# Relative-position attention with a binary feed-forward branch: pairs ordered by half of the query blocks, query and key halves taken straight from PSUM, operands loaded in pieces, first outputs spread over eight pairs

## The chip, the cores and the metric

The kernel runs on one core of one Trainium2 chip. The metric is the device time of one execution in microseconds (us); the time of a kernel is the median of several runs. The core has the engines PE (TensorE: matrix products into PSUM banks), DVE (VectorE), ACT (ScalarE), POOL (GpSimd) and SP (SyncE, which here only issues DMA transfers). Each engine works through its own instructions in order and waits at an instruction until the semaphores that it names are there.

## The reference

The input x is 16 sequences of 512 rows of 128 features. What is computed, cut to what matters:

```python
xn = layernorm(x)
q, k, v = xn' @ Wq + bq, xn' @ Wk + bk, xn' @ Wv + bv      # xn' = layernorm(xn) * g + b; 16 heads of 8
p = sinusoidal(512, 128) @ Wp
content = einsum("bihd,bjhd->bhij", q + u_bias, k)
pos = relative_shift(einsum("bihd,jhd->bhij", q + v_bias, p))
attn = softmax((content + pos) * 8 ** -0.5)
head = einsum("bhij,bjhd->bihd", attn, v)                  # 16 x 16 x 512 x 8
out = x + (head @ Wo + bo) + ffn(xn)
# ffn: [h, -h] @ (+1/-1 weights, 256x512), relu * 2, 512x512, relu * 2, 512x128, scaled by s0, s1, s2
```

## The kernel before

**Three stages.** A prologue computes the projections and the FFN for one sequence b after another and leaves what attention needs in DRAM scratch. An attention loop does all 16 heads. A tail multiplies the summed heads by Wo, adds the residual and stores.

**The prologue.** The FFN of sequence b is ffn_layer (products L640, splits L617 and L618), ffn_last (L674, into the bank a_t) and ffn_out (L685 to L691, which stores x + bo + FFN to res_scr). Between its steps the function more() pops a list of other steps at a fixed rate: norm (L318 to L339), transposed2 (L509, L620, L621), with_bias (L520), project_q (L545), project_k (L565), project_v (L575, L583), and next_quads at the end (L594 to L596). SPAN says over how many of the FFN's sequences the list is spread (12.3), XB how many tiles of x there are (4). PSUM has seven banks in turn: three for those steps (psw, names 0 to 2) and four for the FFN (F_BANKS). Queries and keys are kept as two f16 parts, a rounded one and the rest. A projection is first scaled and biased from PSUM into an f32 tile by ACT (scaled, L528), then halves_to makes the parts: ACT copies (L502) and POOL subtracts (L503).

```python
        def halves_to(src, hi, lo):
            nc.scalar.copy(hi, src)
            return nc.gpsimd.tensor_tensor(lo, src, hi, ALU.subtract)
```

The query tiles are zeroed by POOL (clear_queries, L496), since each 32-row group holds the queries of every second sequence only. ffn_residual loads x again and POOL adds the bias (L661, L662). When the list is empty, more() issues the stores of the query quads (L605, L606) and the loads of the first head.

**The attention loop.** A unit is four queries (of each of four blocks of 128 rows) of all 16 sequences for one head; 16 units make a pair, and two pairs, up = 0 and 1, make a head. Pairs are ordered by head and then by up, 32 in all. e_t holds the exponentials of two pairs in turn. A cycle does two units in the order of STEPS; A and B are score matmuls (scores, L797, L813, L826), F, G, H the maxima (L840, L845), T and N the transposed maxima (L850, L854), X and Y the subtraction of the maximum on PE and the exponential on ACT (L859, L869), V the products with the values for the pair before (weighted, L887, copied out at L896).

```python
STEPS = "N0- A0 B0 G1- H1- X0- F0 Y0- T1- N1- V G0 X1- A1 Y1- H0 T0 B1 F1"
```

In the attention loop, a manual schedule keeps PE, DVE and ACT in the order in which the program states their instructions. POOL and SP are ordered by the framework, which follows program order as far as buffers allow. The rules for what is issued between steps stand in the loop at the end:

```python
                nl = n // UL + 1
                if u % UL == 1 and 2 <= nl < len(loads):
                    if nl % NL == 0:
                        load_head(nl // NL)
                    load_queries(*loads[nl])
```

So every 8 units the queries for the next 8 are loaded into the buffer of the two that comes free (12 transfers of 64 KB: L216 for the content part, L220 and L224 for the two position parts), and every 32 units a head's keys, windows and values (load_head, L202, L205, L207, L208), always all at once.

**Sums and division.** At the end of half a pair, stored_sums (L921 to L931) writes the denominators to a small tile (den, L921) and the unnormalised sums to sum_scr (L926). Some cycles later inverted() takes the reciprocal (L929) and stores it (L931). Once per head divided() reads both back (L942, L943; the reciprocals broadcast to eight rows), multiplies on POOL (L946) and writes the quotients to head_scr (L947).

**The tail.** The last two pairs run last_steps: load_sums (L960) reads the quotients of all other heads, load_rden and divide (L963, L978) finish the first half of the last head, load_res (L970) reads the residuals. For the last pair last_sums multiplies by a selector matrix on PE, so that each denominator stands in the rows of its head (L904), then reciprocal and product on DVE (L906, L907), and last_moved moves the rows into the tile of sums (L914). output_of does four sequences at a time, eight times: products with Wo (L986), the add of the residual (L994), two stores (L997). In the last pair SP is in the manual order too.

The functions follow as they stand in the kernel; the line numbers are those of the profile.

## Time and profile before

| | |
|---|---|
| median of 3 runs | 1370.04 us (1368.51 to 1371.51) |
| the profiled execution | 1368.64 us |
| its span, first to last instruction | 1366.9 us |
| mean granted TensorE clock | 0.985 |
| PE busy | 1289.9 us (94%) |
| DVE busy | 1113.8 us (81%) |
| ACT busy | 882.3 us (65%) |
| POOL busy | 130.7 us (10%) |
| DMA packets, bytes | 243607, 160.22 MB |

The page gives the busy time of each engine over the whole span, and then in 40 slices of 34.2 us, where a digit is the busy share in tenths. A line of a timeline has the start in us from the first instruction, the duration, the engine (SPq is SP's own DMA queue), the line and operation, what is written and read, and in brackets how long the engine stood idle before it and what released it. A source row gives minimum, median and maximum of the durations in ns.

### The profile page before, as it was taken

The page shows a single profiled execution, that of the slowest core. Times are in us where ns is not written, and L with a number is a line of the kernel's source. Part 1 is how long each engine was busy: PE and PEld are TensorE (multiplying, and loading weights), DVE is VectorE, ACT ScalarE, POOL GpSimd, SP SyncE. Part 2 cuts the span into 40 slices and gives each one's busy share as a digit, 9 for nine tenths or more (in the row PEclk, how much of TensorE's full clock was granted, in tenths as well). Part 3 has the DMA queues.
Part 4 walks back from the last instruction along what each step waited for, and adds up shares of the span by engine and source line. Part 5 has one row for each costly group of instructions (what it writes and reads, how often), then busy time and mean ns, then how long its engine had stood idle before and what let it go on. Part 6 is the DMA issues. An engine that isn't in the chain of part 4 may idle for free. (4 is left out here: it accounts for less than half of the span.)

```text
span 1366.9 us, 55407 instructions
## 1 busy us (share of the span) xinstructions
PE 1289.9 (94%) x23061; PEld 952.7 (70%) x23061; DVE 1113.8 (81%) x2723; ACT 882.3 (65%) x1456; POOL 130.7 (10%) x115
## 2 busy tenths in 40 slices
PE   4988889979999999999999999999999999999966
PEld 2545555667777777777777777777777777777735
DVE  8988754678888888888888888888888888788846
ACT  4576668466666666666666666666666666666630
POOL 4243445010000000000000000000000000000011
PEclk9999999999999999999999999999999999999987
DMA  4597869863243323333333323332333353323288
GB/s 117 168 234 198 202 159 264 245 193 89 76 104 79 98 80 92 81 98 90 84 93 89 94 78 97 82 96 77 96 84 93 87 123 86 99 78 81 69 145 190
DMA packets 243607, 160.22 MB, mean 117 GB/s; under 512 B 79510, under 2 KB 227100, under 8 KB 243356
## 3 DMA queue, kind: packets, MB, share of 16 engines
q1 hardware_dynamic: 243356, 156.69, 43.9%
q8 instruction: 180, 2.95, 0.9%
q14 instruction: 71, 0.58, 0.2%
HBM read 96.34 MB, written 59.48 MB: 114 GB/s over the span
## 5 line engine op out<-in xcount | busy, mean ns | idle before, releaser
L869 ACT ACTIVATE e<-s,e_scale 128x512 f32<-128x512 f32 x1024 | 673.1, 686 | 319.9 <-PE s L859 319.5
L840 DVE TENSOR_REDUCE m<-s 128x256 bf16<-128x512 f32 x512 | 351.0, 686 | 132.0 <-PE s L826 131.9
L845 DVE TENSOR_TENSOR m<-s,m 128x256 bf16<-128x256 f32 x1024 | 428.5, 418 | 18.5 <-PE s L826 0.6
L797 PE MATMUL s<-q,k 128*128 128x64 f16 x8192 | 407.0, 193 | 4.0 <-DMA q<-qu_scr 2.1
L859 PE MATMUL s<-ident_b,nm 128*128 128x256 bf16 x2048 | 353.0, 275 | 2.3 <-DVE nm L854 2.3
L813 PE MATMUL s<-q,win 128*128 128x128 f16 (+1 forms) x4096 | 342.6, 206 | 0.0
L797 PEld LDWEIGHTS <-k 128*128 128x128 f16 x8192 | 334.3, 98 | 11.0 <-DMA q<-qu_scr 2.2
L887 PE MATMUL a_t<-e,v 128*9 128x256 f32 x4032 | 267.0, 382 | 0.7 <-ACT e L869 0.6
L813 PEld LDWEIGHTS <-win 128*128 128x128 f16 x4096 | 232.2, 98 | 0.2
L826 PE MATMUL s<-q,win_d 128*128 128x64 f16 x2048 | 227.7, 193 | 0.8 <-DMA q<-qv_scr 0.6
L859 PEld LDWEIGHTS <-nm 128*128 128x128 bf16 x2048 | 145.1, 98 | 117.2 <-DVE m L845 78.8
L854 DVE TENSOR_REDUCE nm<-t_t 128x2 bf16<-128x256 bf16 x512 | 208.8, 408 | 2.4 <-PE t_t L850 2.4
L887 PEld LDWEIGHTS a_t<-e,v 128*9 128x9 f32 x4032 | 86.5, 90 | 81.8 <-issue 2.5
L850 PE MATMUL t_t<-ident_b,m 128*128 128x128 bf16 x1024 | 141.0, 219 | 1.0 <-DVE m L845 0.9
L826 PEld LDWEIGHTS <-win_d 128*128 128x128 f16 x2048 | 130.2, 98 | 1.2 <-issue 1.1
L946 POOL TENSOR_TENSOR raw<-raw,rden 128x512 f32<-128x512 f32 x15 | 19.1, 1273 | 987.6 <-DMA rden<-rden_scr 762.8
L850 PEld LDWEIGHTS <-m 128*128 128x128 bf16 x1024 | 81.0, 97 | 32.7 <-DVE m L845 1.7
L640 PEld LDWEIGHTS <-e 128*128 128x128 f16 x512 | 49.5, 98 | 62.1 <-issue 14.8
L896 ACT COPY av<-a_t 128x256 f32<-128x256 f32 x126 | 47.0, 373 | 32.3 <-PE a_t L887 17.9
L618 DVE SCALAR_TENSOR_TENSOR h2l<-s,h2h 128x512 f16<-128x512 f32 x45 | 30.9, 686 | 37.0 <-ACT h2h L617 36.8
L640 PE MATMUL s<-h1l,e 128*128 128x512 f16 x180 | 47.1, 379 | 0.5 <-DVE h1l L618 0.4
L617 ACT ACTIVATE h2h<-s 128x512 f16<-128x512 f32 x45 | 26.9, 597 | 32.1 <-PE s L640 32.0
(176 smaller groups left out, 905.3 us busy)
## 6 DMA issues: line engine op xcount, KB each, us to landing
q<-qv_scr SPq DMA_DIRECT2D x512, 64.0 KB
q<-qu_scr SPq DMA_DIRECT2D x256, 64.0 KB
qu_scr<-k SPq DMA_DIRECT2D x32, 256.0 KB
k_scr<-hv SPq DMA_DIRECT2D x64, 128.0 KB
qu_scr<-win SPq DMA_DIRECT2D x32, 256.0 KB
qv_scr<-e SPq DMA_DIRECT2D x16, 512.0 KB
k<-k_scr SPq DMA_DIRECT2D x64, 128.0 KB
win<-p_scr SPq DMA_DIRECT2D x64, 79.5 KB
```

The costliest lines, as they stand in the source:

```text
L640: nc.tensor.matmul(ph, lhsT=w[:, t, f * P : (f + 1) * P], rhs=h[t][m], start=(m == 0 and t == 0), stop=(m == 1 and t == n - 1),)
L797: nc.tensor.matmul(sp[:, c % 2, :, :, 4 * g : 4 * g + 4].rearrange("p a r (n m) -> p n (a r) m", m=2), lhsT=kt[:, g, c * P : (c + 1) * P], ...
L813: nc.tensor.matmul(blocks[:, x0 : x0 + (NC + 1) * (len(cs) - 1) + 1 : NC + 1], lhsT=win[h % 2][:, side, y0 : y0 + P], rhs=qp[:, side, :, c ...
L826: nc.tensor.matmul(blocks[:, x0 : x0 + NC + 2 : NC + 1, 2 * t : 2 * t + 2], lhsT=win_d[h % 2][:, t, UP_OFF - 4 * u : WIND - 4 * u], rhs=qd ...
L840: nc.vector.tensor_reduce(st["m"], flat(st["ps"][0]).rearrange("p c x -> p x c"), AX.X, ALU.max)
L845: nc.vector.tensor_tensor(st["m"], flat(st["ps"][1])[:, c], st["m"], ALU.max)
L850: nc.tensor.transpose(st["pt"][:, f, :], st["m"][:, f * P : (f + 1) * P], ident_b)
L854: nc.vector.tensor_reduce(st["nm"], st["pt"], AX.X, ALU.max, negate=True)
L859: nc.tensor.matmul(flat(st["ps"][half])[:, :, f * P : (f + 1) * P], lhsT=st["nm"][:, f : f + 1].to_broadcast([P, P]), rhs=ident_b.unsqueez ...
L869: nc.scalar.activation(st["eT"][:, :, cs, :, i0 : i0 + 4].rearrange("p b c a r -> p (c a) b r"), st["ps"][half].rearrange("p c a r b -> p ...
L887: nc.tensor.matmul(bank[32 * r : 32 * r + VW, g], lhsT=v_t[h % 2][:, v0 : v0 + VW], rhs=pair["eT"][:, b, c], start=(c == 0 and (g == 0 or ...
L896: nc.scalar.copy(pair[half][:, g], bank[:, g])
```

## The change

1. **Order of the pairs.** All 16 heads' first half (up = 0) come first as pairs 0 to 15, then all second halves as pairs 16 to 31. Keys, windows and values are loaded for each pair, into buffers that alternate by pair. The score scratch, the reciprocals and the quotients hold one half at a time.
2. **Operands in pieces.** load_queries, and load_head without the values, return four pieces each; the loop appends them to a list and issues one piece per unit. The values come as one load at the fifth unit of a pair, from a scratch laid out by sequence and then head, which the prologue stores in one run per row.
3. **Content queries.** project_q does two sequences at once in two PSUM banks; qu_scr stores both in one row, so a row group's load also brings the other sequence's queries, and a POOL memset zeroes those right behind the load, in every piece.
4. **Halves from PSUM.** The weights are scaled once (q_mul, k_mul), ACT makes the rounded part with the bias from PSUM, and DVE makes the rest from PSUM (scalar_tensor_tensor; for the position queries in four pieces). The f32 tiles between, POOL's subtraction and two kinds of tile go. Banks: two for q, two for the other steps, three for the FFN. XB becomes 6 and SPAN 13.4. The residuals and the zeroing of the query tiles are placed elsewhere among the FFN's sequences.
5. **Division.** divided() works on one pair, half the size. Reciprocal, its store, the reads with the product, and the last store are four links; each F step of an even unit (one per cycle) runs the next link of every chain under way. For up = 0 and for the last seven heads the quotients go straight to the tile all_sums; for the first nine heads of the second half they go to early_scr and are loaded in one transfer later, as all_sums is in use.
6. **Outputs.** The first half's 16 sequences are done in pairs 17 to 24, two in each: the residual is loaded, two products with Wo go to one half of a_t (first_output), DVE adds into the residual's tile ("o", two buffers), two stores take it out, and the tile after next is loaded behind them. load_last reads the second half's residuals (2 MB) in pair 30. The last pair's denominators go through the selector as before, now also those of the second half of the pair before it; moved() and the output stores use SP's and ACT's queues, and eight calls of last_output end the kernel.

```diff
-    qu_scr = scr("qu_scr", [4, DH * H, B, S, 2], F16)
+    qu_scr = scr("qu_scr", [4, DH * H, B // 2, S, 2], F16)
...
-    v_scr = scr("v_scr", [P, H, B, NC * VW], F32)
-    sum_scr = scr("sum_scr", [H - 1, DH, B, 2, 2 * P], F32)
-    rden_scr = scr("rden_scr", [H, B, 2, 2 * P], F32)
-    head_scr = scr("head_scr", [P - DH, B, 2, 2 * P], F32)
+    v_scr = scr("v_scr", [P, B, H, NC * VW], F32)
+    sum_scr = scr("sum_scr", [H, DH, B, 2 * P], F32)
+    rden_scr = scr("rden_scr", [H, B, 2 * P], F32)
+    early_scr = scr("early_scr", [EARLY * DH, B, 2 * P], F32)
     res_scr = scr("res_scr", [B, S, D], F32)
-    Q_PARTS, K_PARTS = ((0, 2), (1, 3)), ((0, 1), (2, 3))
+    Q_PARTS, P_PARTS, K_PARTS = ((0, 3), (1, 2)), ((0, 2), (1, 3)), ((0, 2), (1, 3))
...
-    def load_head(h):
-        m = h % 2
+    def load_head(h, m):
...
-        nc.sync.dma_start(v_t[m], v_scr[:, h].rearrange("p b f -> p (b f)"))
+        return [lambda n=n: load(n) for n in range(4)]
+    def load_values(h, m):
+        nc.sync.dma_start(v_t[m].rearrange("p (b f) -> p b f", b=B), v_scr[:, :, h])
...
+        def load(n):
...
-                qu[:, n::4, 2 * l * P : 2 * (l + 1) * P],
-            )
+                qu[:, n // 2 :: 2, 2 * l * P : 2 * (l + 1) * P],
+            )
+            nc.gpsimd.memset(qc_t[m][rows_n, :, n // 2, :, 1 - n % 2], 0.0)
...
+        return [lambda n=n: load(n) for n in range(4)]
...
-        def psw(name, banks=(0, 1, 2)):
+        def psw(name, banks=(0, 1)):
...
-        XB = 4
+        XB = 6
...
-        SPAN = 12.3
+        SPAN = 13.4
...
-            nc.vector.tensor_scalar(q_mul, pw[:, 0:1], scale, None, ALU.mult)
+            for t, mul in ((wp_d, k_mul), (wq_d, q_mul), (wk_d, k_mul)):
+                nc.vector.tensor_scalar(t, t, mul, None, ALU.mult)
...
-        def halves_to(src, hi, lo):
-            nc.scalar.copy(hi, src)
-            return nc.gpsimd.tensor_tensor(lo, src, hi, ALU.subtract)
+        def halves_to(src, n, hi, lo):
+            nc.scalar.activation(hi, src, AF.Identity, bias=b_cols[:, n : n + 1])
+            for r in range(4) if len(src.shape) == 4 else [slice(None)]:
+                nc.vector.scalar_tensor_tensor(
+                    lo[:, r], src[:, r], b_cols[:, n : n + 1], hi[:, r], ALU.add, ALU.subtract
+                )
...
+            for n in range(2):
+                nc.tensor.matmul(
+                    q_banks[:, n],
+                    lhsT=wq_d,
...
+            halves_to(q_banks.rearrange("p n j -> p j n"), 0, *qu)
             for m in range(2):
                 for part in Q_PARTS[m]:
-                    nc.sync.dma_start(qu_scr[part, :, b], qu_b[n][m])
...
+            halves_to(
+                q_banks.rearrange("p n (q r) -> p r q n", r=4), 1, *[q[:, :, :, b : b + 2] for q in qv_all]
+            )
...
+            halves_to(pk, 2, *hv)
+            for m in range(2):
+                for part in K_PARTS[m]:
+                    nc.sync.dma_start(k_scr[part, :, b, :], hv[m])
...
-            nc.sync.dma_start(v_scr[:, :, b, :], vb.rearrange("p h c w -> p h (c w)"))
+            nc.sync.dma_start(v_scr[:, b], vb.rearrange("p h c w -> p h (c w)"))
...
-                if b + n + (RB if b else 0) < B:
-                    ffn_residual(b + n + (RB if b else 0))
+            for n in ((0, 1), (2, 3))[b] if b < 2 else (b + 2,):
+                if n < B:
...
-        def last_moved(pair, half, rs):
-            for r in rs:
+        def moved(pair, half, gs, engines):
+            for r in range(4):
                 b = 8 * half + 2 * r
-                nc.sync.dma_start(sums[1][L0:L1, b : b + 2], pair[half][32 * r : 32 * r + DH])
+                engines[r % len(engines)].dma_start(
+                    all_sums[rows_of_head(pair["h"]), b + gs[0] : b + gs[-1] + 1],
+                    pair[half][32 * r : 32 * r + DH, gs[0] : gs[-1] + 1],
+                )
...
             def inverted():
                 nc.vector.reciprocal(den, den)
-                inv = rden_scr[h, bs, up]
-                nc.sync.dma_start(inv.rearrange("b (q m) -> b q m", q=16), den)
-                if h == H - 1:
-                    load_rden(half)
-                elif up == 1 and half == 1:
-                    divided(h)
+                return inverse_stored() if n == 2 * H - 2 else inverse_stored
+            def inverse_stored():
+                nc.sync.dma_start(rden_scr[h, bs].rearrange("b (q m) -> (b q) m", q=16), den)
+                if half == 1:
+                    return lambda: divided(pair, B)
+                if n == 2 * H - 2:
+                    return lambda: divided(pair, B // 2)
...
+            nc.sync.dma_start(raw, sum_scr[h, :, :nb])
+            nc.sync.dma_start(rden, rden_scr[h, :nb].unsqueeze(0).to_broadcast([DH, nb, 2 * P]))
             nc.gpsimd.tensor_tensor(raw, raw, rden, ALU.mult)
-            nc.sync.dma_start(head_scr[h * DH : (h + 1) * DH].rearrange("w b u i -> w b (u i)"), raw)
+            if up and h < EARLY:
+                dst = early_scr[h * DH : (h + 1) * DH]
+            else:
+                dst = all_sums[rows_of_head(h)]
+            def stored():
+                nc.sync.dma_start(dst[:, :nb], raw)
+            return stored
...
+        def load_first(b):
+            if b < B:
+                first_res[b] = wk.tile([P, 2 * P], F32, tag="o", name=f"o_{b}")
+                res_rows(first_res[b], 0, b)
+        def products(dst, b):
...
+        def first_output(b, free):
+            products(a_t[:, free], b)
+            def added():
+                t = first_res.pop(b)
+                nc.vector.tensor_tensor(t, a_t[:, free], t, ALU.add)
+                res_rows(t, 0, b, store=True)
+                load_first(b + 2)
+            return added
...
+        def last_output(b0, step):
+            out_banks.append(out_banks.pop(0))
+            po = out_banks[-1].rearrange("p (b i) -> p b i", b=2)
+            bs = slice(b0, b0 + step + 1, step)
+            for x in range(2):
+                products(po[:, x], b0 + step * x)
+            nc.vector.tensor_tensor(last_res[:, bs], po, last_res[:, bs], ALU.add)
+            for b in (b0, b0 + step) if step > 1 else (slice(b0, b0 + 2),):
+                b = b if step == 1 else slice(b, b + 1)
+                for m in range(2):
+                    (nc.sync, nc.scalar)[m].dma_start(
+                        half_rows(out, 1, m, b),
+                        last_res[64 * m : 64 * m + 64, b].rearrange("p b (k d) -> p (b k) d", d=D),
+                    )
...
-        loads = [(h, l) for h in range(H) for l in range(NL)]
-        units, pairs, later, due, filled = {}, {}, [], [], []
+        loads = [(h, 2 * up + l) for up in range(2) for h in range(H) for l in range(2)]
+        units, pairs, later, due, filled, loading, outputs = {}, {}, [], [], [], [], []
...
-                if u % UL == 1 and 2 <= nl < len(loads):
-                    if nl % NL == 0:
-                        load_head(nl // NL)
-                    load_queries(*loads[nl])
+                if n % UL == 1 and 2 <= nl < len(loads):
+                    loading += load_queries(*loads[nl])
+                if n % UP == 1 and nl + 1 < len(loads):
+                    loading += load_head(loads[nl + 1][0], (n // UP + 1) % 2)
+                if n % UP == 4:
+                    loading.append(lambda h=h, m=n // UP % 2: load_values(h, m))
+                if loading:
+                    loading.pop(0)()
+                if n % 2 and outputs:
+                    filled.append(first_output(*outputs.pop(0)))
...
-                if due and n % 2 == 0:
-                    due.pop()()
+                if filled and n % 2 and n > UP * H:
+                    filled.pop()()
+                if n % 2 == 0:
+                    due = [more for more in (do() for do in due) if more]
...
+                k, pair = k[0], pairs[n]
+                if n == 2 * H - 2 and k == 3:
                     manual.close()
                     manual.enter_context(tc.manual_schedule(engines=ORDERED | {mybir.EngineType.SP}))
+                if n == 2 * H - 1 or (n == 2 * H - 2 and k == 7):
+                    due = [more for more in (do() for do in due) if more]
+                if n == 2 * H - 1 and k == 0:
+                    last_sums(pairs[n - 1], 1, 1)
+                    moved(pairs[n - 1], 1, (0, 1), [nc.sync])
...
+                    weighted(pair, 2 * k + m)
+                if n == 2 * H - 1:
+                    if k % 2 == 0 and k:
+                        last_sums(pair, *divmod(k // 2 - 1, 2))
+                    continue
+                if k == 0 and n == H + 1:
+                    load_first(0)
+                    load_first(1)
+                if k % 4 == 3 and H < n < H + 9:
+                    outputs.append((2 * (n - H - 1) + k // 4, 0))
+                if k == 1 and n == H + 11:
+                    nc.sync.dma_start(all_sums[: EARLY * DH], early_scr)
+                if n < 2 * H - 2:
+                    if k % 4 == 2 and later:
                         due.append(later.pop(0))
-                    if k[0] % 4 == 3:
...
+                    if k % 4 == 3:
+                        later.append(stored_sums(pair, k // 4))
+                elif k in (2, 4):
+                    due.append(later.pop(0))
+                elif k == 3:
+                    later.append(stored_sums(pair, 0))
+                    load_last()
+                elif k == 6:
+                    last_sums(pair, 1, 0)
...
+        moved(pair, 0, (0, 1), [nc.sync, nc.scalar])
+        last_output(0, 1)
+        last_sums(pair, 1, 1)
+        moved(pair, 1, (0,), [nc.sync, nc.scalar])
+        last_output(2, 1)
+        moved(pair, 1, (1,), [nc.sync, nc.scalar])
+        last_output(4, 1)
+        last_output(6, 1)
+        for b in (8, 12, 9, 13):
+            last_output(b, 2)
```

## The prediction

> **What bounds the kernel now.** I read the forty slices of the page first, then busy times by window, the waits, and the timeline of the places that they point at.
>
> ```profile
> PE   4988889979999999999999999999999999999966
> DVE  8988754678888888888888888888888888788846
> ACT  4576668466666666666666666666666666666630
> DMA  4597869863243323333333323332333353323288
> ```
>
> There are three stages. A prologue (projections and FFN) runs up to the first score matmul at 263.9 us (first start of L797). The attention loop runs from the first exponential at 270.4 to the last at 1315.0 (L869): 1044.6 us for 256 cycles of two units. A tail of 51.9 us remains.
>
> ```profile
> 800.00:900.00 100.00, 100.00 (x2094) 77.41 (x2090) 86.60 (x206) 68.72 (x113) 1.27 (x1) 1.00 0.33 87
> 1320.00:1325.00 5.00, 0.42 (x8) 0.00 (x0) 0.00 (x0) 0.00 (x0) 0.00 (x0) 1.00 1.01 162
> 1325.00:1330.00 5.00, 0.00 (x0) 0.00 (x0) 0.00 (x0) 0.00 (x0) 3.05 (x1) 0.51 0.70 128
> ```
>
> Columns: window, length, busy PE, PEld, DVE, ACT, POOL, clock, DMA share, GB/s. In the loop PE is never idle; DVE and ACT have room. A cycle is 4.03 us (score-value steps, L887, start at 1284.76, 1288.79, 1292.83), so a PE microsecond added there costs one, and one that a load comes late costs one. In the tail PE is empty for 10 us while the queues are full:
>
> ```profile
> 1323.86 0.30 SPq L963 DMA_DIRECT2D e<-rden_scr  x1
> 1324.90 0.61 SPq L921 DMA_DIRECT2D den<-av  x1
> 1331.07 0.25 DVE L929 RECIPROCAL den<-den 128x16 f32<-128x16 f32 x1 [17.55 <-DMA den<-av]
> 1333.08 1.19 PE L904 MATMUL t_t<-av,sel 128*128 128x256 f32 x2 [12.66 <-DVE e L906]
> ```
>
> SP stood until 1323.86 for a reciprocal written behind megabytes of reads; the denominators behind it went late, DVE's in-order queue stood 17.6 us for them, and PE 12.7 us for DVE.
>
> **Base of the sum.** The profiled execution took 1368.64 us, 1.7 more than its span, and lies 1.4 below the median. I sum changes on it and add them to the median.
>
> **Tail: -24.** The second half alone is left for the end. Gone are the reads of summed heads (about 2 MB each half) and of 2 MB of residuals inside the tail, half of the 128 output passes (L986, 7.3 us for 64), half of the 4 MB of stores, and the denominators of the second to last pair as a DMA. Followed from the last exponential (ends 1315.7): eight value steps of 0.96 us and three selector matmuls of 0.56 fill PE to about 1325. DVE's reciprocal and multiply (1.74 + 0.43, L906, L907) need one bank each time, so the second pair of them ends near 1323. The moves of that half are issued on two queues (0.65 us each) and land about 2 us later, near 1326.5. Eight outputs of 0.92 us PE and 0.69 us DVE follow, the last waiting for its own move: last add near 1337.5, two issues, 2 to 4 us to land: 1341 to 1343. That is 26 to 28 us against 51.9. I take -24; ends -18 (the 2 MB of residuals, read 20 us ahead, still hold up the moves) and -30.
>
> **First outputs inside the loop: +7.3.** 16 blocks of two fp32 products, 4 passes of 0.114 us: 7.3 us on the full PE. The add of 128x256 (0.42, row L845) fits DVE's idle 0.5 us per cycle; without that cover it costs up to 6 more.
>
> **Operands for every pair: +27.** k, win and win_d are now read 32 times, not 16, v in runs of 144 bytes. The DMA share (0.33) carries it: 17 ns for such a packet in the writes of before, 2048/16 of them 2.2 us. Here a rule speaks against the change. The row: a 64 KB query load takes SP 0.43 us and about 2.0 us to land (worked out from the semaphore times), eight in flight. The Trainium skill (DMA: Bandwidth & Descriptors, Bandwidth) wants transfers of 1 MiB and calls those under 64 KB dominated by descriptors; the Anatomy section gives each some 2 us of fixed cost. If that added up, 13 more transfers per pair would cost 26 us of 32; by the row they cost SP 6 us, beside PE. I take the row: bandwidth isn't the limit, the order in SP's queue is.
>
> ```profile
> 804.96 0.30 SPq L216 DMA_DIRECT2D q<-qu_scr  x1
> 808.07 0.58 SPq L921 DMA_DIRECT2D den<-av  x1
> 808.70 1.52 SPq L926 DMA_DIRECT2D sum_scr<-av  x4
> 810.27 0.31 SPq L224 DMA_DIRECT2D q<-qv_scr  x1
> 821.08 0.30 SPq L216 DMA_DIRECT2D q<-qu_scr  x1
> 837.12 0.61 SPq L943 DMA_DIRECT2D rden<-rden_scr  x1
> 841.69 1.27 POOL L946 TENSOR_TENSOR raw<-raw,rden 128x512 f32<-128x512 f32 x1 [62.54 <-DMA rden<-rden_scr]
> ```
>
> A query buffer comes free at R = 804.96 and its next content is needed 16.1 us later (821.08 is the other buffer's release). Before, loads went out at once. After, as the changed program is built, SP holds ahead of the second set of each pair the denominators (R+3.1) and four sums (to R+5.3), then v 0.6, the first quarter 1.4, the reciprocal's store 0.7, two quarters 2.9, the raw sums 0.5: the read of the reciprocals is issued at R+11.3, the last quarter ends near R+13.3. POOL stands for that read, with the last quarter's zeroing queued behind its multiply, and PE's next scores wait for the zeroing. Issue to multiply was 4.6 us for 256 KB; half the data I take at 3.9. Then 0.65 (half of 1.27) and 0.53 for 512 zeros (row L496): R+16.4 plus a semaphore, 0.4 us late. Ends: nothing (one microsecond better anywhere), 1.5 (v's small runs hold those behind them). 22 pairs without outputs: 8.8.
>
> In eight pairs two output stores and two residual reads enter the same chain. The reads take the buffer that the store has just left, so SP waits for its landing, which lies behind v: 1.0 + 1.0 us and a wait of 1 to 2. With PE's own 0.46 taken off, the last quarter is some 2.7 us late (ends 1 and 4): 21.6. Of before's own late loads (cycles of 4.5 to 4.6 us at every fourth load) about 3 go. Together 8.8 + 21.6 - 3 = +27.
>
> **Prologue: +3, start of attention +1.** Halves are taken from PSUM: ACT loses the three scalings of a block (0.78 to 0.81, L528), POOL all of L503 (63 us), DVE gains per block k 0.60, qu 0.57, qv 4 x 0.34 / 2 (the pace of such rows back to back): 1.85, 30 us in all, in a stage where it is 84 to 90% busy for the first 150 us. What it gets back is its blocking by POOL:
>
> ```profile
> L332 DVE TENSOR_SCALAR step<-step x16: 162/170/3332, 7.2 to 172.7; 128x8 f32<-128x8 f32 x16
> L335 DVE TENSOR_SCALAR xn<-xn,st,root x64: 326/339/1698, 7.9 to 176.5; 128x128 f32<-128x128 f32 x64
> ```
>
> Minimum, median, maximum: the maxima lie under POOL instructions. Durations above the median sum to 37 us over all DVE rows, 21 of them under L503 and L492, which go. The Trainium skill (SBUF — State Buffer, Who interferes with whom) says that a two-port DVE instruction and a GpSimd one exclude each other for the whole of it: by the rule up to 67 us of L503 and L492 could come back, by the row 21. I take 21, so DVE has 9 us more. The queue is spread over 67 calls, not 61.5, and FFN has three banks, not four; the PE-bound end (10.5 us a block from 231) becomes shorter. I take +3; ends -8 (the ACT-POOL chain goes from PE's waits) and +12 (DVE-bound throughout). The loads of the first unit follow next_quads, which moves from 31 us ahead of FFN's end to some 20; copies, eight stores and 12 loads took 25 in a full queue, fuller than it will be: +1, ends -1 and +5. Zeroing of 4 us on POOL and the q tiles' clearing are off the path.
>
> **Sum.** -24 + 7.3 + 27 + 3 + 1 = +14.3 to +14.8: 1383 on the profiled run, 1385 on the median. So the tail's gain is paid back in 30 small waits.
>
> **Rivals.** (a) Faster: the last quarter lands in time. The mechanism is the same chain, SP to POOL to PE, at the ends of the pairs; it decides at zeroing finished by R+16.1, that is reciprocals back within 3.3 us and a residual read that doesn't wait for its store. For it: 128 KB is half of what took 4.6 us, and before's last query issue at R+14 (851.23, needed at 853.3) did no harm. Against: eight pairs have 3 us more in the chain. -24 + 7.3 + 3 + 1 = -13: 1357 (1348 to 1366). (b) Every pair 1.5 us late, since v's small runs push all behind them: 22 x 1.5 = 33 in place of 8.8: 1409. (c) The prologue is held by DVE: +12 in place of +3: 1394, for it 84 to 90% busy before, against it the freed ACT and POOL.
>
> **Numbers.** The forecast case 0.47 (1374 to 1396), (a) 0.33, (b) 0.12, (c) 0.08. Predicted 1385. 1352 to 1404 leaves out the best fifth of (a) and most of (b), under 2 in 10. About 0.2% (2.7 us) is what a measurement of this kernel can tell from no change: 0.06 lies within it, where only part of the waits comes; faster 0.32, slower 0.62.
>
> **What would show it.** Tail from last exponential to end 26 to 28 us. In the waits, PE's score matmul on POOL's zeroing, some 0.4 us in ordinary pairs and 2 to 3 us in pairs 17 to 24; cycles of 4.03 elsewhere. DVE maxima of L332's kind down, first score matmul at 260 to 276. The prediction is wrong if cycles at pair ends stay at 4.03 (then (a)), or if the first score comes beyond 276.

## The result and the profile after

The changed kernel takes 1477.2 us (median of 4 runs, 1472.1 to 1485.66) against 1369.28 us before: 1.079 times as long, 95% interval 1.0756 to 1.0823. The profiled execution took 1485.66 us, with a span of 1483.9. By stages of the two profiled executions (the line numbers from here on are those of the changed kernel unless said otherwise):

| stage | before | after | difference | forecast |
|---|---|---|---|---|
| up to the first exponential | 270.4 | 251.1 | -19.3 | +4 |
| first to last exponential | 1045.3 | 1199.5 | +154.2 | +34 |
| last exponential to the end | 51.2 | 33.2 | -18.0 | -24 |
| span | 1366.9 | 1483.9 | +117.0 | +14 |

So the prologue is better than forecast, the tail somewhat worse, and the loop loses 154 us. Three rows of the page's forty slices:

```profile
PE   6899998899899999999999999898898899979996
DVE  8899666787687778777877787676777778867774
PEclk9999999999999999999999999999999999989998
```

PE no longer shows an unbroken row of nines in the loop. The waits say for what:

```profile
PE s L801 <- POOL q L218: 98.5, 29, 8.5
```

Score matmuls (L801) waited 98.5 us in 29 places for POOL's zeroing of the content queries (L218). With two waits on other releasers there are 31 gaps of PE before L801, 102.4 us; before the change there were four, 4.0 us. All but one stand at the first scores of a pair. Pairs are counted here by their exponentials; the outputs, which the change's pairs 17 to 24 hold counted by their values, then stand in pairs 18 to 25. Here is one wait, at the end of pair 9:

```profile
607.69 0.64 SPq L960 DMA_DIRECT2D rden<-rden_scr  x1
608.44 0.39 SPq L214 DMA_DIRECT2D q<-qu_scr  x1
...
611.31 0.72 POOL L961 TENSOR_TENSOR raw<-raw,rden 128x256 f32<-128x256 f32 x1 [2.77 <-DMA rden<-rden_scr]
612.45 0.66 POOL L218 MEMSET q<- 32x512 f16 x1 [0.41 <-DMA q<-qu_scr]
...
613.16 0.39 PE L801 MATMUL s<-q,k 128*128 128x64 f16 x8 [3.15 <-DMA sums<-raw]
```

The reader is to see the chain: the read of the reciprocals leaves SP at 607.69, ahead of the last piece of the queries; POOL stands for it until 611.31, then multiplies, then zeroes, and PE starts 0.05 us after the zeroing ends (the releaser that the PE line names is a transfer of the same moment). PE had been ready at 610.01. What the wait then costs is in the windows around it (length, busy PE, PEld, DVE, ACT, POOL, granted clock, DMA share, GB/s):

```profile
600.00:610.01 10.01, 10.01 (x210) 7.71 (x202) 8.34 (x20) 7.09 (x12) 2.02 (x3) 1.00 0.53 119
610.19:613.60 3.41, 0.44 (x12) 0.54 (x13) 0.92 (x3) 0.00 (x0) 1.38 (x2) 1.00 0.22 60
613.60:617.01 3.41, 3.41 (x42) 2.11 (x38) 1.98 (x5) 1.27 (x2) 0.00 (x0) 0.50 0.14 32
```

PE is busy again from 613.16, but for 3.41 us the granted clock is 0.50, and 42 matmuls run where some 72 would at the pace of the first row. The pair lasted 37.2 us: 32.2 + 3.15 of waiting + 1.8.

**The sum of the loop.** PE waited 102.4 - 4.0 = 98.4 us more. The cycles with a first output last 4.56 us instead of 4.03 (the eight that no low clock touches), 16 times: 8.5. Of 154.2 us 47.3 are left, 1.5 for each of the 31 waits: the low clock behind them. The clock's own records agree: in the loop it stood at 0.50 for 112.6 us, worth 56.3 us of full clock, against 3.4 us before; part of that fell on time in which PE stood anyway.

### The profile page after: what moved, and what is told of

The parts are those of the page before. It is cut to its first block, busy times and chain, and to the rows that moved or that the text cites. A ratio compares the mean times of both kernels' runs of the same rounds, so it can differ in the third digit from the quotient of the medians.

```text
span 1483.9 us, 56292 instructions
## 1 busy us (share of the span) xinstructions
PE 1332.5 (90%) x23065; PEld 976.8 (66%) x23065; DVE 1131.3 (76%) x2793; ACT 852.5 (57%) x1399; POOL 230.6 (16%) x340
## 3 DMA queue, kind: packets, MB, share of 16 engines
q8 instruction: 181, 2.97, 0.9%
## 4 chain that ended last, share of the span: by engine, by line
PE 63%; SPq 11%; DMA 10%; DVE 8%; POOL 3%; issue 3%; ACT 1%; POOLq 0%; DVEq 0%; ACTq 0%
PE a_t L890 13%; PE s L863 13%; PE s L801 13%; PE s L817 9%; DMA rden<-rden_scr 7%; PE p L626 5%; PE s L830 3%; PE t_t L854 3%; SPq L223 2%; SPq L219 2%; SPq L214 2%; DVE m L844 1%; POOL raw L961 1%; POOL q L218 1%; DVE m L849 1%
## 5 line engine op out<-in xcount | busy, mean ns | idle before, releaser
L801 PE MATMUL s<-q,k 128*128 128x64 f16 x8192 | 413.9, 195 | 104.0 <-POOL q L218 98.5
L801 PEld LDWEIGHTS <-k 128*128 128x128 f16 x8192 | 342.6, 99 | 112.8 <-issue 55.0
L863 PE MATMUL s<-ident_b,nm 128*128 128x256 bf16 x2048 | 364.0, 281 | 2.5 <-issue 1.6
L817 PE MATMUL s<-q,win 128*128 128x128 f16 (+1 forms) x4096 | 348.3, 209 | 0.0
L218 POOL MEMSET q<- 32x512 f16 x256 | 171.5, 670 | 930.6 <-DMA q<-qu_scr 756.0
L890 PE MATMUL a_t<-e,v 128*9 128x256 f32 x4032 | 280.0, 397 | 0.0
L854 PEld LDWEIGHTS <-m 128*128 128x128 bf16 x1024 | 85.9, 100 | 35.0 <-DVE m L849 4.9
L626 PE MATMUL p<-h1l,e 128*128 128x512 f16 x240 | 63.3, 383 | 0.0
L603 ACT ACTIVATE h2h<-p 128x512 f16<-128x512 f32 x60 | 35.7, 597 | 47.1 <-PE p L626 43.8
L626 PE MATMUL p<-h1h,e 128*128 128x512 f16 x240 | 62.2, 379 | 0.0
```

The lines of the kernel that those rows point to most:

```text
L218: nc.gpsimd.memset(qc_t[m][rows_n, :, n // 2, :, 1 - n % 2], 0.0)
L626: nc.tensor.matmul(ph, lhsT=w[:, t, f * P : (f + 1) * P], rhs=h[t][m], start=(m == 0 and t == 0), stop=(m == 1 and t == n - 1),)
L801: nc.tensor.matmul(sp[:, c % 2, :, :, 4 * g : 4 * g + 4].rearrange("p a r (n m) -> p n (a r) m", m=2), lhsT=kt[:, g, c * P : (c + 1) * P], ...
L817: nc.tensor.matmul(blocks[:, x0 : x0 + (NC + 1) * (len(cs) - 1) + 1 : NC + 1], lhsT=win[side_m][:, side, y0 : y0 + P], rhs=qp[:, side, :, ...
L854: nc.tensor.transpose(st["pt"][:, f, :], st["max"][:, f * P : (f + 1) * P], ident_b)
L863: nc.tensor.matmul(flat(st["ps"][half])[:, :, f * P : (f + 1) * P], lhsT=st["nm"][:, f : f + 1].to_broadcast([P, P]), rhs=ident_b.unsqueez ...
```

## The experiments

Theory Q: the order in SP's and POOL's queues makes the waits, and the clock doubles part of them. Rivals: the transfers themselves are slow (B), or POOL's zeroings are the cost (Z). All edits are to the changed kernel, but for e13.

**e1: the division's reads two cycles later.**

```diff
-                    return lambda: divided(pair, B)
+                    last = lambda: divided(pair, B)
+                    return (lambda: lambda: last) if n < 2 * H - 3 else last
```

> The reads and the multiply of the division run two cycles later in every pair but the last three, behind the last piece of the queries. Theory Q (the order in SP's and POOL's queues makes the wait): in the changed kernel's trace the last zeroing always starts when the multiply ends, 0.7 us ahead of PE; without the two reads (1.1 us of issue) and the multiply, the last piece lands some 2.5 us earlier, the 31 stalls of PE fall from 3.3 us to 0.5 to 1, and with them most of the 1.7 us of half clock behind each: about 1375 us (1360 to 1400). Rival B (the transfers themselves are slow, from twice the keys and small runs of the values): the last piece still lands late, 1450 us or more.

Measured 1384.06 us; waits of PE before L801 34.0 us in 19 places, those for POOL:

```profile
PE s L801 <- POOL q L218: 12.0, 7, 5.2
```

Theory Q holds; nothing about the transfers was changed but their order. What is left lies mostly (19.6 us) in pairs 18 to 25.

**e2: the values behind the queries.**

```diff
-                if n % UP == 4:
+                if n % UP == 9:
                     loading.append(lambda h=h, m=n // UP % 2: load_values(h, m))
```

> The values are appended behind the four pieces of the queries instead of ahead of them. Theory Q: the issue of the values (0.6 us) and the wait for a free slot right behind it (about 1 us) leave the chain, stalls fall by some 1.6 us to 1.7, in all 1477 - 31 x (1.6 + 0.5) = about 1412 us (1395 to 1435). Rival B (the small runs of the values hold the queries' packets in the DMA engines): landing of the queries falls by 2 us as well, stalls nearly go, 1370 us or less.

Measured 1379.85 us, better than expected. Pairs 1 to 17 all last 32.2 or 32.3 us; the 28.0 us of waits left before L801 stand in pairs 18 to 25, but for two in pair 0 and one in pair 28. I had overlooked that the edit does two things: the pieces of the queries are now stated one unit earlier, so the reads of the division come behind the last piece as well. It is e1 and e5 that take the two apart.

**e3: no zeroing.**

```diff
-            nc.gpsimd.memset(qc_t[m][rows_n, :, n // 2, :, 1 - n % 2], 0.0)
```

> The zeroing of the other sequence's content queries is left out, so the scores mix two sequences; everything else runs. Theory Q: PE then waits for the last position queries (issued 3.5 us ahead of its start, about 2.2 us to land) instead of for POOL: stalls fall by 1.2 us to 2.1, 1477 - 31 x 1.5 = about 1430 us (1415 to 1450). Rival Z (256 zeroings of 0.67 us on POOL are the cost): stalls nearly go, about 1350 us.

Measured 1451.85 us: 73.9 us of waits remain, now mostly for the loads of the queries themselves (54.6 us). POOL's zeroings are not the cost (Z falls); the last piece is late by itself. The gain was smaller than I expected.

**e4: transposes without a use in the wait.**

```diff
+                if n % UP == 0 and n:
+                    for f in range(24):
+                        nc.tensor.transpose(t_t[:, 2, f % 2], ident_b, ident_b)
```

> 24 transposes without a use (some 3.1 us of PE) are put ahead of each pair's first scores, where PE stands 3.3 us. Theory C (each stall costs twice: the granted clock is 0.50 for 3 us behind it): PE has almost no idle time there, the clock stays at 1.0, and the loop is shorter by up to 31 x 1.6 = 50 us: about 1435 us (1425 to 1450). Rival: the low clock has another cause, and the transposes only fill the wait: 1477 us, or some us more where the stall was shorter than 3.1.

Measured 1464.07 us: the gain is 13, not 42. The 24 transposes took 1.5 us, not 3.1 (with 0.4 of idle time ahead of them), so PE still stood in most pairs. But the clock:

```profile
core 0: 1460.5 us, clock 0.984
```

It was 0.957 in the changed kernel's profile. PE's waits, transposes counted as such (31 x 1.89 + 52.7), came to 111.3 us; of the loop's 129.3 us over before, 107.3 are waits, 8.5 outputs, and 13.5 are left for the clock where 47.3 were (by the clock's records 15.4 us of full clock, where 56.3 were). So the low clock follows from PE standing idle. What is left comes with idle times of 2 to 8 us that stayed behind the transposes, in pairs 18 to 24 and 28 above all. The waits grew by 9 us, part of it in pairs that would have waited less than the transposes take.

**e5: the values in long runs.** The scratch's old layout: loads in runs of 2304 bytes.

```diff
-    v_scr = scr("v_scr", [P, B, H, NC * VW], F32)
+    v_scr = scr("v_scr", [P, H, B, NC * VW], F32)
...
-        nc.sync.dma_start(v_t[m].rearrange("p (b f) -> p b f", b=B), v_scr[:, :, h])
+        nc.sync.dma_start(v_t[m].rearrange("p (b f) -> p b f", b=B), v_scr[:, h])
...
-            nc.sync.dma_start(v_scr[:, b], vb.rearrange("p h c w -> p h (c w)"))
+            nc.sync.dma_start(v_scr[:, :, b], vb.rearrange("p h c w -> p h (c w)"))
```

> Only the scratch of the values goes back to its old layout: loads in runs of 2304 bytes, stores of the prologue in runs of 144. Theory Q: the wait for a free slot behind the values' load (about 1 us) goes, the rest of the chain stays: stalls from 3.3 to 2.3 us, part of them then short enough not to bring the low clock (so far stalls of up to 2.1 us cost 0.2 us more than their length, longer ones 1.8): about 1425 us (1405 to 1445), the prologue within 3 us. Rival B (the small packets hold everything): 1390 us or less.

Measured 1427.33 us, as Q expected. The waits of the ordinary pairs (1 to 17, 26, 27, 29 and 30) have a mean of 1.3 us instead of 2.6: the small runs are part of the delay, by what they do to the transfers right behind them. SP's first issue behind the values takes 0.54 us on average instead of 1.47.

**e6: POOL subtracts again.** halves_to fills an f32 tile from PSUM by ACT, copies, and POOL subtracts.

```diff
-            nc.scalar.activation(hi, src, AF.Identity, bias=b_cols[:, n : n + 1])
...
+            nc.scalar.activation(t, src, AF.Identity, bias=b_cols[:, n : n + 1])
+            nc.scalar.copy(hi, t)
+            nc.gpsimd.tensor_tensor(lo, t, hi, ALU.subtract)
```

> The rest of each half is made by POOL again, from an f32 tile that ACT fills from PSUM (and the tile of the keys' halves has two buffers, as before, to make room); scaled weights, list, spread and banks stay as changed. Theory P (the 18.5 us that the prologue gained come from taking the chain from ACT to POOL and its blocking of DVE out): first score matmul at 258 to 268 instead of 245.4, the total 12 to 20 us longer, 1490 to 1497 us. Rival L (the longer spread of the list, more tiles of x and other banks did it): first score at 243 to 250, total 1477.

Measured 1501.3 us, first score matmul at 273.1: 27.7 us later than in the changed kernel, more than the 18.5 it had gained. The direction is P's; the size is not clean, as one f32 tile stands where before had three.

**e7: first outputs on ACT's queue** (with e2's edit). Stores and reads of res_rows use nc.scalar; reads wait three steps.

```diff
-                load_first(b + 2)
+                reads.append(b + 2)
...
+                if k % 4 == 2 and reads:
+                    load_first(reads.pop(0))
```

> The values behind the queries as in the run that did that alone; the first outputs' stores and residual reads are issued by ACT's queue, and a tile's next read comes some three cycles behind its store instead of at once. Theory Q: SP's queue loses 5.2 us of issue in the pairs with outputs, and the 28 us of stalls and some 10 us behind them that were left in pairs 17 to 25 go, but for PE's own 0.46 us an output: 1345 us (1335 to 1355). Rival A: ACT stands for the store's add and its own issues (8 x 0.65 us a pair) and is late with exponentials, 1360 to 1375 us.

Measured 1367.86 us, 0.9995 times before (0.9978 to 1.0012). That is 23 us above the expectation and in rival A's range, but not for rival A's reason: in the pairs with outputs PE waited only 1.6 us for ACT. **e8** adds the early quotients in four loads:

```diff
-                if k == 1 and n == H + 11:
-                    nc.sync.dma_start(all_sums[: EARLY * DH], early_scr)
+                if k == 6 and H + 10 <= n < H + 14:
+                    b = 4 * (n - H - 10)
+                    nc.sync.dma_start(all_sums[: EARLY * DH, b : b + 4], early_scr[:, b : b + 4])
```

> As the run with outputs on ACT's queue, and the one load of 1.2 MB of the first nine heads' quotients in pair 28, behind which SP stood for 7.5 us, is cut in four of 0.3 MB, one a pair. Theory Q: the 5.7 us that pair 28 was longer fall to 1 or less: 4 to 6 us below the run without this edit, about 1340 us. Rival: the four loads each hold a pair up by 1.5 us, no gain.

Measured 1362.85 us, 0.9963 times before (0.9946 to 0.998), and pair 28 lasts 32.2 us instead of 39.7. Why ACT's queue did so little shows in e8's trace, here in a pair with outputs:

```profile
1002.95 3.37 SPq L936 DMA_DIRECT2D sum_scr<-av  x4
1003.24 1.34 ACTq L983 DMA_DIRECT2D out_dram<-o  x2
```

The four issues of the sums take 1.5 us elsewhere, here 3.37. It isn't that issues take turns: SP's issues of position queries last 0.43 us in the median, with one of ACT's beside them or without. SP waits for ACT's transfers to land:

```profile
SPq L936 <- DMA out_dram<-o: 15.3, 8, 3.2
SPq L223 <- DMA o<-res_scr: 9.3, 6, 3.3
```

In this program the transfers of both queues are given the same eight semaphores in turn. SP's second issue of the sums names the semaphore that ACT's store of 1003.24 holds; that store has landed in full at 1005.33, and SP issues at 1005.35. With the rows of L959, L219 and one more of L936 such waits come to 32.9 us, at the sums and the pieces of the queries above all, where a deadline follows.

**e9: the outputs apart, on SP** (with e2's and e8's loads). One output beside the last step of a pair's values, one beside the second of the next.

```diff
-                if k % 4 == 3 and H < n < H + 9:
-                    outputs.append((2 * (n - H - 1) + k // 4, 0))
+                if k in (2, 7) and reads:
+                    load_first(reads.pop(0))
+                if k == 7 and H < n < H + 9:
+                    outputs.append((2 * (n - H - 1), 0))
+                if k == 1 and H + 1 < n < H + 10:
+                    outputs.append((2 * (n - H - 2) + 1, 1))
```

> The values behind the queries, the early quotients in four loads, and the first outputs back on SP's queue but at other steps: one beside the last step of a pair's values, one beside the second of the next (in the other half of a_t), each next read of a tile three or more cycles behind its store; so nothing of them stands between the denominators of mid-pair and the last piece of the queries. Theory Q: pairs 18 to 25, still 27 us longer together when two queues issued at once, keep only PE's 7.4 us: 1343 us (1337 to 1350). Rival F (SP's queue is full in these pairs wherever the outputs are put, 28 of 32 us with its waits for slots): as on ACT's queue, 1358 to 1368 us.

Measured 1366.98 us: rival F holds. The issues of SP, with what each waits in the queue, add up to 31.6 us in pairs 18 to 24 (59 transfers), of 32.2 that a pair should last (these lasted 36.4 on average); in ordinary pairs to 26.1 (52), before the change to 20.3 (44). With a queue that full, another place for the outputs alone helps little.

**e10: the last moves on ACT** (e9, and moved() of the second to last pair with nc.scalar).

> The same, and the four moves of the second to last pair's second half are issued by ACT instead of SP, where they stood behind the two reads, the multiply's store and their waits. Theory Q: ACT's copy of the last pair (9.4 us late behind these moves, since its tile has two buffers) and PE's wait of 6.8 us for it go: 5 to 6 us below the run without this edit, about 1338 us. Rival: the outputs then wait for the last quotients of that pair's first half instead, gain below 2 us.

Measured 1366.11 us: within 0.1% of e9, no gain. PE's wait fell from 5.3 us to 3.6, and others came behind it.

**e11: the outputs apart and on ACT's queue** (e9 and e7's queue together).

> The placement of the run with the outputs apart (one beside the last step of a pair's values, one beside the second of the next, reads three or more cycles behind), but stores and reads issued by ACT's queue, so that SP's queue, which was full in these pairs, has eight transfers less and ACT issues nothing in the stretch from mid-pair to the last piece. Theory Q with a full queue: the stalls of 1.5 to 3 us in pairs 18 to 25 go, 20 us below the run with them on SP: 1347 us (1340 to 1354). Rival S (the two queues' issues share one generator of descriptors, so an issue on ACT takes SP's time as well): 1360 to 1366 us.

Measured 1350.15 us, 0.9837 times before (0.9817 to 0.9857): faster than both kernels. From pair 1 on PE's waits at L801 are 1.1 us or less, and the loop is 1062.9 us. SP's issues in pairs 18 to 24 come to 25.9 us where e9 had 31.6. SP still waits for ACT's transfers, but now mostly at the windows of the next pair's keys, where no deadline follows soon:

```profile
SPq L197 <- DMA out_dram<-o: 16.6, 7, 3.2
```

**e12** leaves the first outputs out:

> The first half's 16 outputs are left out altogether (products, adds, reads, stores), so half of the output isn't written; values behind the queries, early quotients in four loads. It shows what the order by halves costs without them: pairs 18 to 25 at 32.2 us, 34 us below the run with the outputs apart on SP: about 1333 us (1328 to 1338); where the rest of SP's work makes the stalls there, 1350 us or more.

Measured 1335.02 us: pairs 18 to 24 last 32.2 to 32.5 us. The first outputs cost e11 15 us, of which 8.5 are PE's own by the changed kernel's cycles.

**e13: before, with the halves from PSUM alone,** one sequence at a time as project_q of before does.

```diff
-            scaled(b, 0, pq, tu)
-            scaled(b, 1, pq, two[0][:, :, n])
-            halves_to(tu, *[t[:, :, n] for t in qu_b[n]])
+            halves_to(pq, 0, *[t[:, :, n] for t in qu_b[n]])
...
+            halves_to(pq.rearrange("p (q r) -> p r q", r=4), 1, *[q[:, :, :, b] for q in qv_all])
```

> The kernel before, and only the halves are taken from PSUM by ACT and DVE, with weights scaled once; list, spread, banks, tiles, order and tail stay. Theory P (the way from PSUM alone makes the prologue's gain): first score matmul at 244 to 252 instead of 263.9, the total 12 to 20 us below before, 1350 to 1358 us. Rival L (the list, banks and tiles made it; DVE's 38 us of new work hold the prologue up): first score at 262 to 275, total 1368 us or more.

Measured 1399.1 us, first score at 299.1: 35 us later than before. Both theories missed. The groups by line account for it, this run's first, then the changed kernel's:

```profile
L505 DVE SCALAR_TENSOR_TENSOR e<-s,b_cols,e 128x512 f16<-128x512 f32 x16 | 38.2, 2386 | 28.9 <-ACT e L504 28.9
```

```profile
L509 DVE SCALAR_TENSOR_TENSOR e<-q_banks,b_cols,e 128x256 f16<-128x256 f32 x32 | 13.3, 477 | 1.1 <-ACT e L507 0.8
```

Writing one sequence's position queries means single f16 values 32 bytes apart (DVE also reads the rounded part so): 2386 / 512 = 4.7 ns each. With two sequences at once they lie side by side: 477 / 256 = 1.9 ns. ACT has the same (2432 ns for 512 values, 1198 for 1024). So the way from PSUM pays only with the two banks of project_q.

**e14: the old list** (XB = 4, SPAN = 12.3).

> The changed kernel with four tiles of x and a spread of 12.3 again. Theory P: first score at 243 to 250 (245.4 in the changed kernel), total as changed, 1470 to 1485 us. Rival L: first score 8 us later or more, total 1485 us or more.

Measured 1472.96 us, first score at 243.5: list and tiles are not the cause (L falls).

**e15: e11 with e1's edit.**

> The best version so far (values behind the queries, early quotients in four loads, outputs apart and on ACT's queue), and the division's reads two cycles later. Theory Q: the last 0.3 to 0.6 us in every second ordinary pair go, some 3 us in all: 1347 us (1343 to 1350). Rival: with the values behind, the division stood behind the last piece already, and later it meets the next pair's loads: no change or up to 5 us more.

Measured 1350.71 us: no change. With the values behind the queries the division's place costs nothing more.

## Why the prediction was wrong

It named the wait, its place and its chain, and gave it under a fifth of its price: 27 us for operands, where the waits took 98.4 and the low clock behind them 47.3. Two steps failed: the length of the waits in the sum of the chain, and the step that prices a microsecond of waiting at one.

- **Late operands, forecast +27.** From PE's need at 610.01 the forecast's clock starts at R = 593.9. Denominators were issued at R+3.4 (forecast R+3.1), sums done at R+5.8 (5.3), but the read of the reciprocals left at R+13.8 instead of R+11.3. The queries' pieces went slower: the first quarter took 2.3 us instead of 1.4, the next two 3.9 instead of 2.9, with two issues of 1.34 and 1.55 us among them where the others take 0.4. I had taken these for waits until one of eight transfers in flight has landed, but the last transfers with the semaphores of those two issues had landed at 599.93 and 600.21, before the issues began (600.45 and 603.73); e5 ties the first of them to the values ahead of it, and what holds the second stays open. From that read to the multiply it took 3.6 us (forecast 3.9), multiply and zeroing 1.8 with the pause between instead of 1.2. That made 3.15 us of the forecast's 0.4, and its upper end was 1.5. I had put the small runs of the values only into that end and into rival (b); e5 shows that they are half of an ordinary pair's wait (1.3 us are left of 2.6), e1 that the division's place alone is nearly all of it. The two overlap: either edit lets the last piece be in time in many pairs. In the eight pairs with outputs the wait was 2.9 to 5.6 us (forecast 2.7 with ends 1 and 4), as SP's queue was full (e9). One wait had no term at all: behind the load of the early quotients in pair 28, SP stood 7.1 us and PE 8.5, and the pair lasted 44.8 us. e8 shows that it goes when that load is cut in four.
- **A microsecond late costs one.** This is the step that failed by itself: 31 waits of mostly over 2 us cost 1.5 more each through the clock, 47 us that the sum didn't have. The trace of before had it: a single wait of 2.1 us, and behind it

```profile
1181.50:1185.00 3.50, 3.50 (x38) 1.61 (x34) 1.87 (x4) 1.35 (x3) 0.00 (x0) 0.54 0.44 117
```

  in a pair that lasted 36.3 us. I had taken the pair for a late load and had not divided it.
- **First outputs, +7.3.** 8.5, about right; but their transfers cost far more than their matmuls.
- **Prologue and start, forecast +4, measured -19.3.** DVE's work did grow, 195.0 us to 203.0 (forecast +9), and the first of the two maxima fell as said, from 3332 ns; the second, 1698 before, did not:

```profile
L338 DVE TENSOR_SCALAR step<-step x16: 148/160/882, 7.2 to 146.8; 128x8 f32<-128x8 f32 x16
L341 DVE TENSOR_SCALAR xn<-xn,st,root x64: 309/339/2011, 7.8 to 148.6; 128x128 f32<-128x128 f32 x64
```

  The 2011 ns lie under POOL's addition of a residual (L650) and the zeroing behind it; of L341's instructions four last over 500 ns, where ten did before. What failed is that I added DVE's work to a stage and left its idle time as it was: the idle time fell from 69 to 42 us, as PE and DVE no longer stood behind the chain from ACT to POOL. Windows of the changed kernel:

```profile
60.00:100.00 40.00, 36.74 (x244) 21.60 (x243) 38.75 (x127) 23.00 (x42) 6.62 (x9) 1.00 0.59 191
100.00:150.00 50.00, 47.69 (x293) 27.18 (x292) 48.41 (x180) 29.36 (x52) 5.66 (x7) 1.00 0.49 160
```

  Before, DVE was busy 34.84 and 42.12 us there and PE 34.80 and 44.01. The end at -8 that I gave to this chain was the right side, and too short. e6, e13 and e14 together leave the halves from PSUM of two sequences at once as its cause; what the banks, the scaled weights and the new places of the residuals and the zeroing did was not tried.
- **Tail, forecast -24, measured -18.** One wait has the size of the difference, of the kind that the forecast had found in the tail of before:

```profile
1454.92 0.58 SPq L960 DMA_DIRECT2D rden<-rden_scr  x1
1458.46 0.66 SPq L968 DMA_DIRECT2D sums<-raw  x1
1459.17 4.11 SPq L923 DMA_DIRECT2D sums<-av  x6
...
1463.38 0.37 ACT L899 COPY av<-a_t 128x256 f32<-128x256 f32 x1 [8.30 <-DMA sums<-av]
1463.80 1.22 PE L915 MATMUL t_t<-av,sel 128*128 128x256 f32 x2 [5.69 <-ACT av L899]
```

  SP stood for a multiply, the moves behind it went late, ACT had no tile for its copy, and PE waited 5.7 us. Taking these moves off SP alone gained nothing (e10): it wasn't the only late thing.
- **Rivals.** Forecast (0.47) and (a) both had the size of the wait below the truth; (b) (0.12) had one of its causes and half its length, and no clock.

## What to carry to other kernels

Where PE is full, price a wait as its length plus what the clock takes behind it (1.7 us here, once some 2 us of idle time fall into one piece of 3.4), and look for one such wait in the trace you have before you call a late load cheap. Add up the issue times of a queue over a period: at 26 of 32 us, transfers without a deadline ahead of those with one make the period late, and moving them behind (e1, e2) is worth more than making one of them faster (e5). And when a stage's busiest engine gets more work, ask what its idle time was waiting for before adding the work to the stage.

## What the runs showed of the hardware

- **The clock.** The stretches at 0.50 inside a loop begin whole multiples of 3.413 us apart, in each profile that has more than one of them (25 in the changed kernel's). So I cut each loop into pieces of that length on the same grid and took PE's idle time in every piece that ran at full clock (e4's transposes count as work). With 0.3 to 1.8 us idle the next piece was at full clock, 320 times of 320; with 2.0 us or more it was at 0.50, 139 times of 139; between 1.8 and 2.0 us 12 times of 27. So two waits of about the same length can have different prices. The 3.15 us of pair 9 (above) left 2.97 us idle in one piece. The 3.29 us at the end of pair 13 fell on two pieces, with 1.43 and 1.87 us idle, and cost 0.2 us more than their length:

```profile
753.57:756.98 3.41, 1.98 (x42) 1.48 (x34) 2.54 (x7) 1.76 (x3) 0.67 (x1) 1.00 0.53 153
756.98:760.39 3.41, 1.54 (x34) 1.56 (x34) 0.76 (x2) 0.15 (x1) 1.38 (x2) 1.00 0.22 59
760.39:763.80 3.41, 3.41 (x80) 2.65 (x78) 2.63 (x8) 2.78 (x5) 0.00 (x0) 1.00 0.07 10
```

  The Trainium skill (TensorE: Matmul & The Clock Gate, HAM oscillation) warns of idle gaps over some 3.4 us. By that rule three of the ordinary pairs' waits (3.56, 3.60 and 4.40 us) would have cost more than their length; 13 did, from 2.29 us on, so 3.4 is no safe limit.
- **Two queues.** The Trainium skill (DMA: Bandwidth & Descriptors, Issuing engines are not separate DMA queues) says that a second issuing engine saves only the time to initiate. Here that was worth 17 us where SP's queue was full (e9 to e11). In e8 much of it was lost, as SP's next issues waited for transfers of ACT's to land (32.9 us of such waits).
- **Single f16 values, 32 bytes apart,** cost DVE 4.7 ns each, and ACT 4.8 (e13), where pairs side by side cost 1.9 and 1.2 (changed kernel).
